# Conditional layer and quantised FFN on one core: where the weights' powers are formed, a GpSimd product and a bound matmul moved

## The chip, the cores and the metric

The kernel runs on one core of one Trainium2 chip. The metric is the device time of the whole program in microseconds (us); lower is better. TensorE (PE in the profile) does the matrix products, VectorE (DVE), ScalarE (ACT) and GpSimd (POOL) the element-wise work, and SyncE (SP) issues the transfers. SBUF is the on-chip memory, PSUM the smaller one that TensorE writes.

## The reference

```python
# x (64, 64, 1024): batch, channel, feature; condition (64,) in 0..15; weights (16, 64, 64)
W = weights[condition]
h = einsum('bct,bcd->bdt', x, W)                    # first product: one 64x64 matrix a batch
w = (unpack6(qweight) - zero_point) * scale         # (1024, 1024), 6-bit integers, one zero point
                                                    # and one scale for each output feature
out = x + einsum('bsk,nk->bsn', h, w) + bias        # second product, bias and residual
```

All tensors are float32, the packed weights int32.

## The kernel before

**Tiling.** Two batches make a pair: 2 x 64 channels lie on the 128 partitions, with the 1024 features along the free axis. There are 32 pairs, and two pairs make a group. For each pair, `stage1` computes h into a PSUM tile `ph` (features on partitions, the channels of both batches along the free axis), and `stage2` multiplies it with the unpacked integers `q` (`qT`) into the PSUM tile `po` (128 x 1024, two banks of 512). Both operands of a product are float16. Precision is kept by splitting each value into a high and a low half: `hh` and `hl` for h, `hf`/`lf` stacked as `xa` for x, a high and a low table `tab` for the weights. So the second product of a pair is 32 matmuls of 128x512 columns: 8 feature tiles, two halves (`hh`, `hl`), two banks.

**Powers.** Values are scaled by a power of two before they are split. `powers(sums, up, down)` (L130 to L138) takes a bound that TensorE has put in PSUM and writes two tiles: `down`, the inverse power by which the operand is multiplied, and `up`, the power that is multiplied back. For the weights of each condition, `weights_powers` makes `wdn` and `wup`, both in SBUF, from the PSUM tile `pw`; `weights_scaled` (GpSimd) multiplies the weights by `wdn`; `weights_high` (ScalarE) and `weights_low` (VectorE) make the table `tab` of it. `weights_hot` and `weights_of_batches` bring `wup` of every batch's condition to the tile `wupb`: a diagonal product `up_k` of `wup` and the identity `eye`, a reduction `up_1`, a row tile `up_w`, an indicator `hot`, and one matmul. `wupb` enters the factor `u` of a group (`unscales`), with which `po` is multiplied at the end.

**Zero point.** The zero point's share is `zt = zero point * sum over features of h` for each pair, made by ScalarE. From pair 4 on it uses `zsc` = zero point times scale, one product on GpSimd (L633), and GpSimd subtracts it from the residual. Pairs 0 to 3 (`early_zero_points`, `early_minus`, `early_res`, `early_add`) use the plain zero point on VectorE: `early_minus` is po * u - zt in PSUM, `early_res` multiplies by the scale into an SBUF tile `res`, and GpSimd adds that later.

**PSUM.** `po` has two buffers, one for even and one for odd pairs; a pair's second product waits until the pair two before has been read out of its buffer. All small matmul results (`pw`, `pl`, `pu`, `pt`, `pb_`) share one pool of two buffers.

**Order.** The order on each engine is written out by hand; each engine executes its own queue in order, and the calls in the program are its order. The main loop `window(p)` covers pairs from 3 on. Ahead of it stands a start-up in which the weights' tables don't exist yet: pairs 0 and 1 run their first product in float32 with plain weights `wbd` (`early_stage1`, bounds by `early_bounds`, powers by `early_scales`, halves by `early_high` and `early_low`). In the meantime the integers are unpacked (`unpack`, VectorE), the table is built, and group 1 (pairs 2 and 3) is prepared: `stacked_high` (ScalarE) and `stacked_low` (VectorE, reads x and `xa`) write `xa` directly, where later groups go through SBUF and transfers (`split_1`, `split_2`, `stack_high`, `stack_low`). `select_pair(n, nc.gpsimd)` copies the two weight matrices of a pair out of `tab` into `wst`; `stage1(n)` reads that. The end of the start-up, in the order of the calls:

```python
    weights_low()
    ...
    for n in range(2, 4):
        select_pair(n, nc.gpsimd)
    nc.gpsimd.tensor_tensor(zsc, zsb, scb, ALU.mult)
    for n in range(4, 8):
        select_pair(n, nc.gpsimd)
```

Of the kernel before, what the change touches and what calls it, by code (L numbers as in the profile page):

```python
# [8 lines left out]
F32 = mybir.dt.float32  # L9
F16 = mybir.dt.float16  # L10
BF = mybir.dt.bfloat16
# [3 lines left out]
ALU = mybir.AluOpType  # L15
AX = mybir.AxisListType
# [13 lines left out]
def adaln_ffn(ctx: ExitStack, tc: tile.TileContext, x, cond, cw, qw, ws, wz, bias, out):  # L30
    nc = tc.nc
    B, C, T = x.shape
    _, NK, D = cw.shape
    N = qw.shape[2]
    P = 128
    NP = B // 2
    NG = NP // 2
    KT = T // P
# [6 lines left out]
    const = ctx.enter_context(tc.tile_pool(name="const", bufs=1))  # L45
# [34 lines left out]
    cb = const.tile([NK, B], I32, name="cb")  # L80
# [39 lines left out]
    spread = const.tile([NK, P], BF, name="spread")  # L120
# [3 lines left out]
    kio = const.tile([NK, 1], F32, name="kio")  # L124
# [3 lines left out]
    eye = const.tile([P, P], BF, name="eye")  # L128
    nc.vector.tensor_scalar(eye, off, 0, None, ALU.is_equal)

    def powers(sums, up, down, least=True):

        if least:
            nc.vector.tensor_scalar(sums, sums, LEAST, None, ALU.max)
        nc.vector.tensor_scalar(
            down.bitcast(I32), sums.bitcast(I32), EXPONENT, EXPONENT, ALU.bitwise_and, ALU.bitwise_xor
        )
        nc.vector.tensor_scalar(up.bitcast(I32), sums.bitcast(I32), EXPONENT, None, ALU.bitwise_and)  # L138
# [5 lines left out]
    def unpack(kt, n=1):  # L144

        w = kt if kt < 2 else kt - 2 if kt < 6 else kt - 4
        to, of_ = q16[:, kt : kt + n, :], qr[:, w : w + n, :]
        if kt in (2, 3, 6, 7):
            nc.vector.tensor_scalar(to, of_, 6 if kt < 4 else 8, 63, ALU.logical_shift_right, ALU.bitwise_and)
        else:  # L150
            nc.vector.tensor_scalar(to, of_, 63, None, ALU.bitwise_and)


    tab = const.tile([P, NK, 2, D], F16, name="tab")
    wup = const.tile([P, NK], F32, name="wup")
    wupb = const.tile([P, NP], F32, name="wupb")
    wdn = const.tile([P, NK], F32, name="wdn")
    wsc = qp.tile([P, NK, D], F32, name="wsc", bufs=1)
    wmx = const.tile([C, NK], BF, name="wmx")
    tmp = {}  # L160
# [4 lines left out]
    def weights_turn():  # L165
        pt = ps_s.tile([NK, C], F32, name="pt", tag="s")
        nc.tensor.matmul(pt, lhsT=wmx, rhs=eye[LO, LO], start=True, stop=True)
        tmp["pt"] = pt

    def weights_diagonal():  # L170
        most = const.tile([NK, 1], F32, name="most")
        nc.vector.tensor_reduce(most, tmp["pt"], AX.X, ALU.max)
        diag = const.tile([NK, NK], BF, name="diag")
        nc.vector.tensor_scalar(diag, eye[0:NK, 0:NK], most[:, 0:1], None, ALU.mult)
        tmp["diag"] = diag
# [4 lines left out]
        tmp["pw"] = pw  # L180

    def weights_powers():
        powers(tmp["pw"], wup, wdn)

    def weights_scaled():
        nc.gpsimd.tensor_tensor(wsc, w32, wdn.unsqueeze(2).to_broadcast([P, NK, D]), ALU.mult)  # L186
# [4 lines left out]
    def weights_low():  # L191
        nc.vector.tensor_tensor(tab[:, :, 1, :], wsc, tab[:, :, 0, :], ALU.subtract)

    def weights_hot():

        hot = const.tile([NK, B], BF, name="hot")
        nc.vector.tensor_scalar(hot, cb, kio[:, 0:1], None, ALU.is_equal)
        up_k = const.tile([NK, NK], F32, name="up_k")
        nc.vector.tensor_tensor(up_k, wup[0:NK, :], eye[0:NK, 0:NK], ALU.mult)
        up_1 = const.tile([NK, 1], F32, name="up_1")  # L200
        nc.vector.tensor_reduce(up_1, up_k, AX.X, ALU.add)
        up_w = const.tile([NK, P], BF, name="up_w")
        nc.vector.tensor_scalar(up_w, spread, up_1[:, 0:1], None, ALU.mult)
        tmp["hot"] = up_w, hot

    def weights_of_batches():
        up_w, hot = tmp["hot"]
        pb_ = ps_s.tile([P, B], F32, name="pb_", tag="s")
        nc.tensor.matmul(pb_, lhsT=up_w, rhs=hot, start=True, stop=True)
        for j, h in enumerate((LO, HI)):  # L210
            nc.vector.tensor_scalar(
                wupb[h], pb_.rearrange("p (i j) -> p i j", j=2)[h, :, j], 1.0 / LARGEST, None, ALU.mult
            )
# [4 lines left out]
    def conditions_of(p, eng=nc.sync):  # L218
        conditions[p] = [
            eng.value_load(cb[0:1, 2 * p + j : 2 * p + j + 1], min_val=0, max_val=NK - 1) for j in range(2)  # L220
        ]

    def select_pair(p, eng=nc.sync):
        g, i = divmod(p, 2)
        if i == 0:
            wsts[g] = sp.tile([P, 2, 2, 2, D], F16, name="wst")
        if p not in conditions:
            conditions_of(p, eng)
        for j, k in enumerate(conditions[p]):
            to, of_ = wsts[g][:, i, :, j, :], tab[:, ds(k, 1), :, :].rearrange("p o a d -> p (o a) d")  # L230
            if eng is nc.sync:
                eng.dma_start(to, of_)
            else:
                eng.tensor_copy(to, of_)
# [9 lines left out]
    def magnitudes(g, i):  # L244
        if g not in st:
            st[g] = {
                "l1": sp.tile([P, 2], BF, name="l1"),
                "u": sp.tile([P, 2], F32, name="u"),
                "hs": sp.tile([P, 2], F32, name="hs"),
                "xs": sp.tile([P, 2], F32, name="xs"),  # L250
                "up": sp.tile([P, 2], F32, name="up"),
                "down": sp.tile([P, 2], F32, name="down"),
                "hf": ap.tile([P, 2, T], F16, name="hf"),
                "lf": ap.tile([P, 2, T], F16, name="lf"),
                "xa": ap.tile([P, 2, 2, T], F16, name="xa"),
            }
        junk = ap.tile([P, T], BF, name="junk", bufs=1)
        nc.scalar.activation(junk, xts[g][:, i, :], AF.Abs, accum_out=st[g]["l1"][:, i : i + 1])  # L258
# [9 lines left out]
    def unscales(g):  # L268
        nc.vector.scalar_tensor_tensor(st[g]["u"], st[g]["up"], 0.25 / QUNIT, wupb[:, 2 * g : 2 * g + 2], ALU.mult, ALU.mult)
# [112 lines left out]
    def early_weights(p):  # L382

        wl = const.tile([P, 1], F32, name=f"wl{p}")
        nc.vector.tensor_reduce(wl, wbd[:, p, :], AX.X, ALU.max, apply_absolute_value=True)
        nc.vector.tensor_scalar(wm[:, p, :], half, wl[:, 0:1], None, ALU.mult)
# [17 lines left out]
    def early_bounds(p, parts):  # L404
        pl = ps_s.tile([P, 2], F32, name="pl", tag="s")
        for n in range(parts):
            nc.tensor.matmul(pl, lhsT=all_ones, rhs=pb[:, p, n, :], start=(n == 0), stop=(n == parts - 1))  # L407
        tmp["pl"] = pl
# [4 lines left out]
    def early_unscales(p):  # L413
        for j, h in enumerate((LO, HI)):
            nc.vector.tensor_scalar(st[0]["u"][h, p : p + 1], updown[h, p, 0, j : j + 1], 0.5 / QUNIT, None, ALU.mult)

    def early_stage1(p, ph, kts=range(KT)):
        for kt in kts:
            nc.tensor.matmul(  # L419
                ph[:, kt % ph.shape[1], :, :], lhsT=xts[0][:, p, ts(kt, P)], rhs=wbd[:, p, :], start=True, stop=True  # L420
            )
# [22 lines left out]
    def early_zero_points(p):  # L444
        g, i = divmod(p, 2)
        zt = ap.tile([P, N], F32, name="zt", bufs=3)
        nc.scalar.activation(zt, zsb, AF.Copy, scale=st[g]["hs"][:, i : i + 1])  # L447
        tmp["zt", p] = zt
# [64 lines left out]
    def stage2_tiles(p, kts, ks=range(2)):  # L513
        if p not in pos:
            pos[p] = ps_o[1 + p % 2].tile([P, N], F32, name="po", tag="po")
        products(pos[p], p, kts, ks, BANKS, BANKS)
# [50 lines left out]
    ph1 = ps_o[0].tile([P, KT, 2, D], F32, name="ph")  # L567
# [12 lines left out]
    early_rows(0, 0)  # L580
    early_rows(0, 1)
    early_stage1(0, ph0b, range(4, KT))
    early_stage1(1, ph1, range(0, 2))
    early_bounds(0, 2)
    early_scales(0)
    early_high(0, ph0a, LOWER)
    early_high(0, ph0b, UPPER)
    early_weights(1)
    early_stage1(1, ph1, range(2, KT))
    unpack(0)  # L590
    unpack(1)
    early_low(0, ph0a, LOWER)
# [3 lines left out]
    early_low(0, ph0b, UPPER)  # L596
    weights_turn()
    weights_diagonal()
    unpack(4, 2)
    stage2_tiles(0, range(0, 2), [1])  # L600
    early_rows(1, 0)
# [5 lines left out]
    early_bounds(1, 1)  # L607
    early_scales(1)
    weights_powers()
    weights_scaled()  # L610
    magnitudes(1, 0)
    early_high(1, ph1, slice(0, KT))
    stage2_tiles(0, range(4, 6))
# [11 lines left out]
    early_feature_sums(1)  # L625
    magnitudes(1, 1)
    early_zero_points(0)
    weights_low()
    unpacking.close()
    late = ctx.enter_context(tc.tile_pool(name="late", bufs=1))  # L630
    for n in range(2, 4):
        select_pair(n, nc.gpsimd)
    nc.gpsimd.tensor_tensor(zsc, zsb, scb, ALU.mult)  # L633
    for n in range(4, 8):
        select_pair(n, nc.gpsimd)


# [1 line left out]
    stage2_tiles(1, range(0, 4), [1])  # L639
    bounds(1, SECOND)  # L640
    scales(1, SECOND)
    early_unscales(0)
    early_unscales(1)
    weights_hot()
    early_minus(0)
    early_res(0)
    stage2_tiles(1, range(4, 7))
# [10 lines left out]
    stacked_low(1, 1, 1)  # L658
    weights_of_batches()
    unscales(1)  # L660


    sums_high(1)
# [167 lines left out]
```

## Time and profile before

| what | us |
|---|---|
| median of 3 runs | 271.44 (270.45 to 272.37) |
| the profiled execution | 271.85 |
| its span, first to last instruction | 270.1 |
| mean granted TensorE clock | 0.993 of full |
| a pair in the steady part (from one `stage1` to the next, 93.11 to 100.95) | 7.84 |

The profile is of one execution. Its span is what the instructions cover; the 1.75 us between span and time lie around it. An engine's row gives its busy time, its share of the span and its number of instructions. Lines of a timeline give the start in us, the duration, the engine, the line of the program, the operation, the output and inputs by their names, the count, and, in brackets, how long the engine was idle before it and what released it. Lines of the list of waits read: total us, times, longest. Lines of windows give the stretch, its length, the busy time of PE, PEld, DVE, ACT and POOL with their instructions, the granted clock, the share of the DMA engines and GB/s.

### The profile page before, as it was taken

How to read it: one execution, taken by the hardware profiler on the slowest of the kernel's cores; microseconds unless marked ns; L12 is line 12 of the kernel's file. 1: busy time of each engine (PE TensorE's matmuls, PEld its weight loads, DVE VectorE, ACT ScalarE, POOL GpSimd, SP SyncE). 2: the span in 40 equal slices, each digit the busy share in tenths (PEclk: the TensorE clock that was granted, in tenths of full speed). 3: DMA queues.
4: the chain of work that ended last, by engine and by line, in shares of the span. 5: the costliest groups of instructions: out<-in, count | busy, mean ns of one | idle time of the engine just before them, and what ended most of it. 6: DMA issues, size and time to landing. Idle time of an engine off the chain costs nothing.

```text
span 270.1 us, 5703 instructions
## 1 busy us (share of the span) xinstructions
PE 261.8 (97%) x2158; PEld 139.9 (52%) x2158; DVE 204.1 (76%) x269; ACT 161.2 (60%) x287; POOL 172.2 (64%) x100
## 2 busy tenths in 40 slices
PE   7997899999999999999999999999999999999993
PEld 7554446445555545555554555555455555545553
DVE  4779999597795959869595986959598695955543
ACT  3799399776565667656566765656676565634100
POOL 3027017959599595969959596895919386595100
PEclk9999799999999999999999999999999999999999
DMA  6993047966667797596965797667966664551212
GB/s 213 341 407 132 1 94 234 268 178 187 198 175 245 225 281 219 120 317 176 302 184 175 233 273 231 174 230 248 272 220 187 203 179 144 161 158 78 80 53 103
DMA packets 31820, 53.34 MB, mean 197 GB/s; under 512 B 15024, under 2 KB 15280, under 8 KB 31792
## 3 DMA queue, kind: packets, MB, share of 16 engines
q1 hardware_dynamic: 31760, 52.96, 63.9%
q8 instruction: 17, 0.28, 0.4%
q14 instruction: 11, 0.09, 0.1%
q10 hardware_dynamic: 32, 0.00, 0.0%
HBM read 19.93 MB, written 16.78 MB: 136 GB/s over the span
## 4 chain that ended last, share of the span: by engine, by line
PE 94%; DMA 2%; DVE 1%; SPq 1%; ACT 0%; issue 0%
PE po L503 80%; PE ph L479 10%; PE pe L503 3%; DMA xt<-in_x_dram 2%; PE ph L419 1%; PE pu L350 1%; DVE po L452 0%; DVE res L458 0%; SPq L65 0%; SPq L86 0%; ACT hh L491 0%; DVE pe L544 0%; DVE xt L549 0%; PE pu L441 0%; PE pl L407 0%
## 5 line engine op out<-in xcount | busy, mean ns | idle before, releaser
L503 PE MATMUL po<-q,hh 128*128 128x512 f16 x496 | 120.0, 382 | 2.3 <-DVE res L458 2.3
L503 PE MATMUL po<-q,hl 128*128 128x512 f16 x496 | 118.5, 379 | 0.0
L539 POOL TENSOR_TENSOR xt<-xt,zt 128x1024 f32<-128x1024 f32 x28 | 78.5, 2822 | 49.3 <-ACT zt L537 49.3
L503 PEld LDWEIGHTS <-hl 128*128 128x128 f16 x520 | 50.8, 98 | 59.8 <-issue 0.4
L491 ACT CAST hh<-ph 128x1024 f16<-128x1024 f32 (+1 forms) x31 | 30.4, 984 | 83.7 <-PE ph L479 41.9
L503 PEld LDWEIGHTS <-hh 128*128 128x128 f16 x520 | 48.7, 98 | 54.9 <-ACT zt L447 2.4
L532 POOL TENSOR_TENSOR xt<-xt,bib 128x1024 f32<-128x1024 f32 x32 | 74.5, 2355 | 1.9 <-issue 1.9
L544 DVE SCALAR_TENSOR_TENSOR po<-po,u,scb 128x1024 f32<-128x1024 f32 x27 | 34.7, 1286 | 49.6 <-PE po L503 49.6
L292 DVE SCALAR_TENSOR_TENSOR lf<-xt,down,hf 128x1024 f16<-128x1024 f32 x28 | 60.1, 2184 | 0.2 <-ACT hf L282 0.2
L495 DVE TENSOR_TENSOR hl<-ph,hh 128x1024 f16<-128x1024 f32 x30 | 36.4, 1215 | 0.1
L479 PEld LDWEIGHTS <-xa 128*128 128x128 f16 x960 | 32.2, 98 | 7.2
L549 DVE TENSOR_TENSOR xt<-po,xt 128x1024 f32<-128x1024 f32 x27 | 33.1, 1225 | 1.9
L479 PE MATMUL ph<-wst,xa 128*128 128x64 f16 x960 | 33.0, 193 | 0.0
L258 ACT ACTIVATE junk<-xt 128x1024 bf16<-128x1024 f32 x30 | 31.7, 1056 | 0.8
L282 ACT ACTIVATE hf<-xt,down 128x1024 f16<-128x1024 f32 x28 | 31.9, 1143 | 0.0
L537 ACT ACTIVATE zt<-zsc,hs 128x1024 f32<-128x1024 f32 x28 | 30.5, 1138 | 0.0
L343 ACT ACTIVATE xh<-xh,xs 64x1 f16<-64x1 f16 x52 | 12.4, 287 | 0.5
L468 POOL TENSOR_TENSOR xt<-xt,res 128x1024 f32<-128x1024 f32 x4 | 9.4, 2360 | 0.0
L339 POOL TENSOR_TENSOR xh<-xs,xh 64x2 f16<-64x2 f32 x4 | 0.8, 194 | 10.7 <-ACT xh L333 10.6
L186 POOL TENSOR_TENSOR wsc<-w,wdn 128x1024 f32<-128x1024 f32 x1 | 1.9, 1902 | 8.3 <-DVE wup L138 8.3
L503 PE MATMUL pe<-q,hh 128*128 128x256 f16 (+1 forms) x24 | 6.6, 308 | 0.0
L503 PE MATMUL pe<-q,hl 128*128 128x256 f16 (+1 forms) x24 | 6.5, 308 | 0.0
(88 smaller groups left out, 123.4 us busy)
## 6 DMA issues: line engine op xcount, KB each, us to landing
out_dram<-xt SPq DMA_DIRECT2D x31, 512.0 KB, 3.0
xt<-in_x_dram SPq DMA_DIRECT2D x14, 1024.0 KB, 7.9
xa<-hf SPq DMA_DIRECT2D x26, 256.0 KB, 3.8
xa<-lf SPq DMA_DIRECT2D x26, 256.0 KB, 3.8
xt<-in_x_dram SPq DMA_DIRECT2D x3, 512.0 KB, 7.8
wst<-tab SPq DMA_DIRECT2D x48, 32.0 KB, 3.2
w<-in_L_cond_weights_dram SPq DMA_DIRECT2D x2, 256.0 KB, 5.9
xt<-in_x_dram SPq DMA_DIRECT2D x2, 256.0 KB, 3.7
```

The lines of the kernel that those rows point to most:

```text
L258: nc.scalar.activation(junk, xts[g][:, i, :], AF.Abs, accum_out=st[g]["l1"][:, i : i + 1])
L282: nc.scalar.activation(st[g]["hf"][:, i, ts_], xts[g][:, i, ts_], AF.Copy, scale=st[g]["down"][:, i : i + 1], accum_out=st[g]["xs"][:, i : ...
L292: nc.vector.scalar_tensor_tensor(st[g]["lf"][:, i, ts_], xts[g][:, i, ts_], st[g]["down"][:, i : i + 1], st[g]["hf"][:, i, ts_], ALU.mult, ...
L479: nc.tensor.matmul(ph[:, kt, j, :], lhsT=st[g]["xa"][:, i, j, ts(kt, P)], rhs=wsts[g][:, i, a, j, :], start=(a == 0), stop=(a == 1),)
L491: nc.scalar.copy(hs_pair[p][0][:, kts, :], ph[:, kts, :])
L495: nc.vector.tensor_tensor(hl[:, kts, :], ph[:, kts, :], hh[:, kts, :], ALU.subtract)
L503: nc.tensor.matmul(po[:, a], lhsT=hs_pair[p][k][:, kt, :], rhs=qT[:, kt, c], start=(kt == 0 and k == 0), stop=(kt == KT - 1 and k == 1),)
L532: nc.gpsimd.tensor_tensor(xt, xt, bib, ALU.add)
L537: nc.scalar.activation(zt, zsc, AF.Copy, scale=st[g]["hs"][:, i : i + 1])
L539: nc.gpsimd.tensor_tensor(xt, xt, zt, ALU.subtract)
L544: nc.vector.scalar_tensor_tensor(po, po, st[g]["u"][:, i : i + 1], scb[:, cols], ALU.mult, ALU.mult)
L549: nc.vector.tensor_tensor(xts[g][:, i, cols], po, xts[g][:, i, cols], ALU.add)
```

## The change

`wup` is no longer written to SBUF: `weights_powers` forms that power in place, in the PSUM tile `pw`, and `weights_own`, called right behind `weights_scaled`, multiplies the diagonal and reduces it there. What was one function `weights_hot` becomes three, called at different places: `weights_hot` (the indicator) behind `weights_diagonal`, `weights_own`, and `weights_up` (the row tile) ahead of `weights_low`. `early_unscales(0)` moves ahead of `weights_low`, `early_unscales(1)` behind `unscales(1)`. GpSimd's `zsc` product comes after the copies of pair 2, ahead of those of pair 3, instead of after both. On TensorE, `early_bounds(0, 2)` comes ahead of all eight feature tiles of `early_stage1(1, ph1)`, instead of after the first two.

```diff
-    wup = const.tile([P, NK], F32, name="wup")
...
     def weights_powers():
-        powers(tmp["pw"], wup, wdn)
+
+        powers(tmp["pw"], tmp["pw"], wdn)
...
     def weights_hot():
 
-        hot = const.tile([NK, B], BF, name="hot")
-        nc.vector.tensor_scalar(hot, cb, kio[:, 0:1], None, ALU.is_equal)
-        up_k = const.tile([NK, NK], F32, name="up_k")
-        nc.vector.tensor_tensor(up_k, wup[0:NK, :], eye[0:NK, 0:NK], ALU.mult)
-        up_1 = const.tile([NK, 1], F32, name="up_1")
-        nc.vector.tensor_reduce(up_1, up_k, AX.X, ALU.add)
-        up_w = const.tile([NK, P], BF, name="up_w")
-        nc.vector.tensor_scalar(up_w, spread, up_1[:, 0:1], None, ALU.mult)
-        tmp["hot"] = up_w, hot
+        tmp["hot"] = const.tile([NK, B], BF, name="hot")
+        nc.vector.tensor_scalar(tmp["hot"], cb, kio[:, 0:1], None, ALU.is_equal)
+
+    def weights_own():
+
+        up_k = tmp["pw"][0:NK, :]
+        nc.vector.tensor_tensor(up_k, up_k, eye[0:NK, 0:NK], ALU.mult)
+        tmp["up_1"] = const.tile([NK, 1], F32, name="up_1")
+        nc.vector.tensor_reduce(tmp["up_1"], up_k, AX.X, ALU.add)
+
+    def weights_up():
+        tmp["up_w"] = const.tile([NK, P], BF, name="up_w")
+        nc.vector.tensor_scalar(tmp["up_w"], spread, tmp["up_1"][:, 0:1], None, ALU.mult)
 
     def weights_of_batches():
-        up_w, hot = tmp["hot"]
+
         pb_ = ps_s.tile([P, B], F32, name="pb_", tag="s")
-        nc.tensor.matmul(pb_, lhsT=up_w, rhs=hot, start=True, stop=True)
+        nc.tensor.matmul(pb_, lhsT=tmp["up_w"], rhs=tmp["hot"], start=True, stop=True)
...
     early_stage1(0, ph0b, range(4, KT))
-    early_stage1(1, ph1, range(0, 2))
     early_bounds(0, 2)
     early_scales(0)
     early_high(0, ph0a, LOWER)
     early_high(0, ph0b, UPPER)
     early_weights(1)
-    early_stage1(1, ph1, range(2, KT))
+    early_stage1(1, ph1)
...
     weights_diagonal()
+    weights_hot()
     unpack(4, 2)
...
     weights_scaled()
+    weights_own()
     magnitudes(1, 0)
...
     early_zero_points(0)
+    early_unscales(0)
+    weights_up()
     weights_low()
...
-    for n in range(2, 4):
-        select_pair(n, nc.gpsimd)
+    select_pair(2, nc.gpsimd)
     nc.gpsimd.tensor_tensor(zsc, zsb, scb, ALU.mult)
-    for n in range(4, 8):
+    for n in range(3, 8):
         select_pair(n, nc.gpsimd)
...
     scales(1, SECOND)
-    early_unscales(0)
-    early_unscales(1)
-    weights_hot()
     early_minus(0)
...
     unscales(1)
+    early_unscales(1)
```

## The prediction

> **What bounds the kernel now.** I read the page's busy shares first, then the list of waits of TensorE, then the timelines of TensorE, VectorE and GpSimd around the one long wait, then the windows there. The chance bounds below use 1% (2.7 us), about what a measurement of this kernel can tell from no change.
>
> ```profile
> PE 261.8 (97%) x2158; PEld 139.9 (52%) x2158; DVE 204.1 (76%) x269; ACT 161.2 (60%) x287; POOL 172.2 (64%) x100
> ...
> PEclk9999799999999999999999999999999999999999
> ```
>
> TensorE is busy 97% of the 270.1 us span, so time can only come from its gaps or from its clock. The clock digit falls once, in the fifth slice (27.0 to 33.8 us). The list of TensorE's waits holds three entries:
>
> ```profile
> PE po L503 <- DVE res L458: 2.3, 1, 2.3
> PE pc L562 <- DVE one L106: 1.1, 1, 1.1
> PE ph L419 <- DMA xt<-in_x_dram: 0.8, 2, 0.5
> ```
>
> The last two lie before 7.7 us (start-up, first loads). The first is the target: pair 2's second product waits until `early_res(0)` has read pair 0's PSUM, which both pairs use in turn. TensorE's timeline there:
>
> ```profile
> 25.40 0.20 PE L209 MATMUL pb__625<-hot,up_w 16*128 16x64 bf16 x1
> 27.92 3.41 PE L503 MATMUL po<-q,hh 128*128 128x512 f16 x8 [2.31 <-DVE res L458]
> 31.16 1.89 PE L503 MATMUL po<-q,hl 128*128 128x512 f16 x8
> ```
>
> Eight hh matmuls take 3.24 us from start to start (27.92 to 31.16), where eight hl take 1.73 (31.16 to 32.89). The windows say why:
>
> ```profile
> 27.90:31.20 3.30, 3.28 (x9) 1.19 (x10) 3.24 (x3) 1.46 (x5) 0.39 (x2) 0.52 0.00 0
> 31.20:32.90 1.70, 1.70 (x10) 0.76 (x9) 1.62 (x5) 0.00 (x0) 0.00 (x0) 1.00 0.00 0
> ```
>
> Column seven is the granted clock: 0.52 behind the gap, 1.00 after. So the wait costs twice: 2.3 us idle and 3.24 - 1.73 = 1.5 us of half clock. Why VectorE is late, from its timeline and GpSimd's:
>
> ```profile
> 22.48 2.34 DVE L199 TENSOR_TENSOR up_k<-wup,eye 16x16 f32<-16x16 f32 x1
> 24.86 0.16 DVE L201 TENSOR_REDUCE up<-up_k 16x1 f32<-16x16 f32 x1
> 25.06 0.26 DVE L203 TENSOR_SCALAR up_w<-spread,up 16x128 bf16<-16x128 bf16 x1
> 25.24 1.27 DVE L452 SCALAR_TENSOR_TENSOR po<-po,u,zt 128x1024 f32<-128x1024 f32 x1
> 26.55 1.23 DVE L458 TENSOR_TENSOR res<-po,scb 128x1024 f32<-128x1024 f32 x1
> ...
> 22.45 2.35 POOL L633 TENSOR_TENSOR zsc<-zsb,scb 128x1024 f32<-128x1024 f32 x1
> ```
>
> A 16x16 product, where other tiny operations take some 0.16, lasts 2.34 us: exactly GpSimd's zsc product (22.45 to 24.80). VectorE then runs in order: up_1, up_w, `early_minus(0)`, `early_res(0)`, and TensorE starts 0.14 after res.
>
> **What the Trainium skill says.** "SBUF — State Buffer", section "Who interferes with whom": a VectorE instruction with two SBUF inputs contends with a GpSimd instruction that reads SBUF, and the second to start blocks fully; with at most one SBUF input (outside its two-port modes) it doesn't. The trace agrees: up_k reads wup and eye, both in SBUF, and lasts as long as zsc, while `early_minus(0)` (PSUM and SBUF) beside GpSimd's copies takes its plain 1.27. "TensorE: Matmul & The Clock Gate", section "What's actually happening", lets the clock halve after an idle window of about 3.4 us; here 2.3 us of idling sufficed for about 3.3 us at half. So I take small waits as free of it and anything near 2 us as at risk.
>
> **The change part by part.**
>
> *Powers in PSUM (`weights_powers`, `weights_own`).* The write of wup becomes an in-place write of pw, one instruction for one (0.16). up_k and the reduction move from 22.5 to behind wdn's power at 14.2, on the same VectorE queue. up_k there has one SBUF input (eye), at most 0.2, and the reduction takes 0.16. VectorE idles 1.18 us until 15.56 at that place, waiting for `bounds(1, FIRST)`, so 0.4 is hidden; uncovered it would cost those 0.4. The tile pw is held until about 14.8; the next tile in its buffer is written at 15.33. Bounds: 0 to 0.4, taken 0.
>
> *hot* (0.24, pitch 0.16) moves ahead of unpack(4, 2). VectorE is full there (9.06 to 13.7), but see the next edit: 0.
>
> *Bound of pair 0 ahead of pair 1's first product.* Its inputs are ready at 6.99 (row L402), TensorE is free at 7.19 and idles till 7.68 for pair 1's load. So the two bound matmuls (8.20 now) run at about 7.2 in that gap, and the powers, `early_high(0)` and VectorE's unpacking come up to 1 us sooner. On TensorE itself only the 0.06 that these took disappears: everything from 7.68 to 25.3 is matmul behind matmul. If the inputs were late, pair 1's product would wait behind them; 0.2 of slack. Taken -0.07.
>
> *early_unscales(0) and weights_up* move from behind `scales(1, SECOND)` to ahead of `weights_low`: two at 0.155 and one at 0.18 make 0.5. Queued behind them: `weights_low` (20.20 now, 20.6 then, tab ready at 21.86), so GpSimd's copies for pair 2 end at 22.4, where stage1(2) starts at 23.5: hidden. Also `scales(1, SECOND)`, 0.43 later, and so ScalarE's stacked_high(1, 1): 21.73 becomes 22.16, ending at 24.66; stage1_high(2) starts at about 24.7 instead of 24.64. No TensorE time.
>
> *zsc ahead of pair 3's copies.* GpSimd: tab 21.9, two copies to 22.4, zsc to 24.7, ten copies at 0.24 to 27.2. Pair 3's are wanted at 29. No DMA and nothing of SP moves in any part.
>
> *The sum.* VectorE after scales(1, SECOND) at 22.1: minus(0) to 23.4, res(0) to 24.65. TensorE, without the wait for up_w and 0.07 earlier, is ready for pair 2's product at about 25.4, so the wait for res goes and the clock stays up. What is late next is hl of pair 2: stacked_low(1, 1, 0), two SBUF inputs, begins at 24.67 at the very end of zsc (24.7) and among copies of 0.24; then stage1_low(2), 1.26. It ends at 27.2 with no contention, at 27.5 with one copy ahead; TensorE wants it at 25.4 + 1.73 = 27.1 and starts 0.14 after its end. So hl begins at 27.35 to 27.65 instead of 31.16: 3.5 to 3.8 gained. Behind it: stacked_low(1, 1, 1) ends at 28.5 to 28.9 for stage1(3) at 29.1 to 29.4. early_unscales(1) (0.31, now behind unscales(1)) and minus(1) end at 30.7, 0.6 after the bounds(2) matmul (30.1), but ScalarE's stage1_high(3) ends only at 31.0, so split_1(2, 0) loses 0.1. split_2(2, 0) runs at 32.85, some 0.4 later against TensorE than now; its DMAs (issue to landing 2.2 to 2.4) had 0.3 of slack to stage1(4) at 40.86. So another 0.1 to 0.2 may be lost there. I take 3.6: the profiled execution (271.85, 1.75 around its span) becomes 268.25. The shown median is 271.44, 0.4 lower; less 3.6 it is 267.8.
>
> **The rivals.**
>
> *Forecast (0.62):* the wait and the half clock go, small new waits of 0.2 to 0.9 remain: gain 3.0 to 3.9, 267.5 to 268.4. For it: every one of the steps above has its row. Against: the new margins are a few tenths.
>
> *The wait turns into one for hl of pair 2 (0.20):* more copies of GpSimd get ahead of stacked_low(1, 1, 0), or both of the two-input operations block, and hl starts 1 to 2 us late with some of the half clock: gain 1.2 to 2.7, about 269.5. For it: in the steady windows the second `split_2` lasts up to 3.44 instead of 1.28 beside GpSimd's products. Against: a copy is 0.24, not 2.35, and the lock changes hands after each instruction there.
>
> *Slower (0.08):* GpSimd keeps its read interface through all ten copies, 2.4 us. Place: stacked_low(1, 1, 0). hl would end at 29.7, TensorE idle from 27.1 to 29.85 and again at half clock for 1.55: pair 2's first bank ends at 33.1 instead of 32.89, 271.7. It decides from a wait of about 2.3 us on; a second such wait with its clock loss at stage1(4), as VectorE's lag reaches the DMAs, would bring 274 and over (half of this chance).
>
> *It doesn't do what it says (0.06):* the in-place power in PSUM still blocks, or res(0) waits for something else in its memory: about 271.
>
> *More (0.04):* also the other executions lose more in that gap than the profiled one: 266.8.
>
> **How the numbers follow.** The forecast's 267.8, median against median. The range leaves out the worst of the slower and the best of the rest: 266.6 to 270.3. Faster by over 1% means below 268.7: nearly all of the forecast, the last case, a few of the second: 0.68. Slower by over 1%: 0.04. Within: 0.28.
>
> **What would show it.** Right: TensorE's list of waits without res L458; clock 1.00 from 25 to 32; up_k some 0.17 long at 14.5; res(0) ending at 24.7; po of pair 2 starting at 25.4; hl beginning near 27.5; from stage1(4) on the same 7.9 us a pair, some 3.6 earlier. Wrong: a stacked_low above 1.6 us, a low clock digit after 25 us, a new wait for hl, xa or a DMA of over 0.7 us.

## The result, and the profile after

The changed kernel takes 268.75 us (median of 5, 267.94 to 269.37) where the kernel before, run beside it, takes 271.86 (median of 5, 270.45 to 272.58): 3.1 us less, ratio 0.989 with a 95% interval of 0.9851 to 0.9928. A second comparison (e11 below) gave 268.26 against 271.73, ratio 0.9863 (0.9824 to 0.9901). The forecast was 3.6 less.

The page of the profiled execution (269.19 us, span 267.4):

```profile
PE 260.4 (97%) x2158; PEld 139.5 (52%) x2158; DVE 200.1 (75%) x269; ACT 161.2 (60%) x287; POOL 174.6 (65%) x100
...
PEclk9999999999999999999999999999999999999999
```

TensorE's share is still 97%, the low clock digit is gone, and VectorE is busy 4 us less with as many instructions: the time in which an instruction stands blocked counts as busy, and up_k alone gave back 2.2. Most of the rest is the product that makes `lf` in the steady part (60.1 us in all before, 58.0 now). TensorE's entries in the list of waits:

```profile
PE ph L423 <- DMA xt<-in_x_dram: 1.2, 3, 0.6
PE pc L566 <- DVE one L106: 1.1, 1, 1.1
PE ph L483 <- DMA xa<-lf: 0.6, 1, 0.6
```

The wait for res is not there. A new one is: `stage1(6)` waits for its stacking transfer. TensorE's timeline at the old and at the new place, and two windows (the clock is the seventh column):

```profile
25.96 0.20 PE L213 MATMUL pb__621<-hot,up_w 16*128 16x64 bf16 x1
26.09 1.90 PE L507 MATMUL po<-q,hh 128*128 128x512 f16 x8
27.87 1.90 PE L507 MATMUL po<-q,hl 128*128 128x512 f16 x8
...
49.93 0.22 PE L483 MATMUL ph<-wst,xa 128*128 128x64 f16 x2
50.76 1.03 PE L483 MATMUL ph<-wst,xa 128*128 128x64 f16 x30 [0.61 <-DMA xa<-lf]
```

```profile
26.00:28.00 2.00, 2.00 (x11) 0.86 (x11) 1.94 (x3) 1.98 (x3) 2.00 (x7) 1.00 0.02 8
28.00:30.00 2.00, 2.00 (x22) 1.07 (x21) 1.87 (x6) 1.92 (x6) 1.69 (x4) 1.00 0.00 0
```

Pair 2's product follows the matmul of `weights_of_batches` after 0.13 instead of 2.52 us, at full clock; its hh half takes 1.78 from start to start. In this execution the load of pair 1 landed 0.7 us later than in the one shown before, so everything up to here stands 0.56 later (pair 0's second product starts at 10.24 instead of 9.68). hl starts 3.29 earlier, 3.85 if that is taken off; of this the wait at stage1(6) gives back about 0.7. VectorE and GpSimd:

```profile
14.99 0.17 DVE L202 TENSOR_TENSOR pw<-pw,eye 16x16 f32<-16x16 f32 x1
...
22.59 1.28 DVE L456 SCALAR_TENSOR_TENSOR po<-po,u,zt 128x1024 f32<-128x1024 f32 x1
23.91 1.23 DVE L462 TENSOR_TENSOR res<-po,scb 128x1024 f32<-128x1024 f32 x1
25.16 1.39 DVE L319 SCALAR_TENSOR_TENSOR xa<-xt,down,xa 64x1024 f16<-64x1024 f32 x1
26.59 1.23 DVE L499 TENSOR_TENSOR hl<-ph,hh 128x1024 f16<-128x1024 f32 x1
...
22.89 2.37 POOL L639 TENSOR_TENSOR zsc<-zsb,scb 128x1024 f32<-128x1024 f32 x1
25.19 4.40 POOL L238 COPY wst<-tab 128x128 f16 x10
```

up_k, the product of pw with eye, takes 0.17 us; res ends at 25.14, ahead of TensorE's need at 26.09. The two-input stacked_low right behind zsc lasts 1.39 instead of 1.28, so it lost 0.1, and hl ends at 27.82, just when TensorE wants it. The blocking has changed sides: GpSimd's ten copies take 4.40 us, at 0.24 each they would take 2.4. Two of them, at 25.42 and at 28.08, stand for 1.29 and 1.28 us, about as long as the two products of stacked_low that they meet.

### The profile page after: what moved, and what is told of

The parts are those of the page before. It is cut to its first block, busy times and chain, and to the rows that moved or that the text cites. A ratio compares the mean times of both kernels' runs of the same rounds, so it can differ in the third digit from the quotient of the medians.

```text
span 267.4 us, 5704 instructions
## 1 busy us (share of the span) xinstructions
PE 260.4 (97%) x2158; PEld 139.5 (52%) x2158; DVE 200.1 (75%) x269; ACT 161.2 (60%) x287; POOL 174.6 (65%) x100
## 4 chain that ended last, share of the span: by engine, by line
PE 82%; DVE 9%; DMA 4%; issue 1%; ACT 1%; SPq 1%; DVEq 0%
PE po L507 69%; PE ph L483 9%; PE pe L507 3%; DMA xa<-lf 2%; DMA xt<-in_x_dram 2%; DVE lf L296 2%; DVE xa L319 1%; DVE hl L499 1%; DVE po L456 1%; ACT xa L311 1%; DVE res L462 1%; PE ph L423 1%; DVE hl L438 0%; PE pu L354 0%; DVE tab L192 0%
## 5 line engine op out<-in xcount | busy, mean ns | idle before, releaser
L507 PE MATMUL po<-q,hh 128*128 128x512 f16 x496 | 118.4, 379 | 0.0
L296 DVE SCALAR_TENSOR_TENSOR lf<-xt,down,hf 128x1024 f16<-128x1024 f32 x28 | 58.0, 2108 | 0.0
L238 POOL COPY wst<-tab 128x128 f16 x12 | 4.9, 454 | 5.5 <-DVE tab L192 5.5
```

Of the source, the lines that this page charges most:

```text
L296: nc.vector.scalar_tensor_tensor(st[g]["lf"][:, i, ts_], xts[g][:, i, ts_], st[g]["down"][:, i : i + 1], st[g]["hf"][:, i, ts_], ALU.mult, ...
L507: nc.tensor.matmul(po[:, a], lhsT=hs_pair[p][k][:, kt, :], rhs=qT[:, kt, c], start=(kt == 0 and k == 0), stop=(kt == KT - 1 and k == 1),)
```

## The experiments

Each kernel ran beside the kernel before; those of one group (e1 to e4; e5 to e8; e9 to e11; e12) on one chip.

| run | us, median | before | ratio, 95% interval |
|---|---|---|---|
| e1 zsc late only | 268.86 | 272.50 | 0.9878 (0.9840 to 0.9915) |
| e2 gap filled | 270.98 | 272.50 | 0.9951 (0.9934 to 0.9967) |
| e3 power in SBUF | 267.97 | 272.50 | 0.9843 (0.9811 to 0.9875) |
| e4 one load early | 268.22 | 272.50 | 0.9845 (0.9814 to 0.9876) |
| e5 zsc at its old place | 268.61 | 272.10 | 0.9870 (0.9841 to 0.9899) |
| e6 bound at its old place | 268.64 | 272.10 | 0.9876 (0.9846 to 0.9907) |
| e7 one product more | 269.48 | 272.10 | 0.9902 (0.9865 to 0.9938) |
| e8 two products more | 270.99 | 272.10 | 0.9954 (0.9939 to 0.9970) |
| e9 two loads early | 267.96 | 271.73 | 0.9843 (0.9808 to 0.9878) |
| e10 the same, zsc late | 268.79 | 271.73 | 0.9875 (0.9840 to 0.9911) |
| e11 the changed kernel | 268.26 | 271.73 | 0.9863 (0.9824 to 0.9901) |
| e12 three products more | 272.75 | 271.82 | 1.0023 (1.0005 to 1.0040) |

**e1: is the lock the cause?** The kernel before, with one line moved.

```diff
-    nc.gpsimd.tensor_tensor(zsc, zsb, scb, ALU.mult)
...
     sums_low(1, nc.gpsimd)
+    nc.gpsimd.tensor_tensor(zsc, zsb, scb, ALU.mult)
```

Expected: 

> The kernel before with one edit: GpSimd's zsc product goes behind the zero-point sums of group 1 (about 30 us), so nothing with two SBUF inputs meets it; wup stays in SBUF, up_k and everything else stay where they are. Theory 1 (the 2.3 us wait comes from up_k blocked by zsc): up_k falls from 2.34 us to 0.2 to 0.5 (a copy of GpSimd may still be ahead), early_res(0) ends at 25.5 to 25.9 instead of 27.78, no half clock, then a wait for hl of pair 2 of 0.6 to 1.0: gain 2.5 to 3.2 us, nearly all of the change's 3.1. Theory 2 (the gain comes from the shorter work of VectorE ahead of early_minus(0) and the earlier bound, the lock is incidental): up_k stays above 1.5 us or the gain is below 1 us.

Measured: 3.6 us less than before; 2.5 to 3.2 was expected. From VectorE's and TensorE's timelines of e1:

```profile
22.46 0.26 DVE L199 TENSOR_TENSOR up_k<-wup,eye 16x16 f32<-16x16 f32 x1
24.44 1.23 DVE L458 TENSOR_TENSOR res<-po,scb 128x1024 f32<-128x1024 f32 x1
...
28.29 1.90 PE L503 MATMUL po<-q,hl 128*128 128x512 f16 x8 [0.59 <-DVE hl L495]
```

The same up_k, at the same place, with the same two inputs in SBUF, takes 0.26 instead of 2.34 us once zsc is away. That is theory 1, and the move of this one line brings as much as the whole change, within the intervals; what the rest of the change saves on VectorE shows here as the wait of 0.59 for hl.

**e2: does the gap cost a second time?** The kernel before, with dummy matmuls in the gap.

```diff
     early_minus(1)
+    fill = ps_s.tile([P, P], F32, name="fill", tag="s")
+    for _ in range(38):
+        nc.tensor.matmul(fill, lhsT=dummy, rhs=dummy, start=True, stop=True)
     stage2_bank(2, 0)
```

Expected: 

> The kernel before with 38 dummy matmuls of 128x128 (about 2.1 us, result unused) put on TensorE into the gap between the matmul of weights_of_batches and pair 2's second product; the wait for early_res(0) stays. Theory 1 (the wait costs twice, by idling and by the half clock behind it): the clock stays at 1.00 from 27.9 to 31.2, eight hh take 1.73 instead of 3.24 us, and the gain is about 1.5 us minus a wait for hl of pair 2 that now shows (hl ends at 30.34, wanted at 29.65: 0.8): 0.5 to 1.5 us. Theory 2 (the half clock is of the time of the run, or of the operands, not of the gap): the low clock stays and nothing is gained, or up to 0.1 is lost.

Measured: 1.5 us less. TensorE's timeline of e2:

```profile
25.18 2.29 PE L668 MATMUL fill<-dummy 128*128 128x128 bf16 x38
27.56 1.89 PE L503 MATMUL po<-q,hh 128*128 128x512 f16 x8
30.04 1.90 PE L503 MATMUL po<-q,hl 128*128 128x512 f16 x8 [0.59 <-DVE hl L495]
```

With TensorE kept busy through the gap, hh runs at full speed and then waits for hl. Without the dummies the half clock had covered that wait. The mean granted clock of every execution says more. In the kernel before, over all its 88 executions in the four groups, it is 0.990 to 0.994 in 53 (median 272.74 us) and 0.997 to 1.0 in 35 (median 271.46); nothing lies between. With the gap filled all 18 executions are at 0.997 or above. So the half clock belongs to the gap, but it comes in about three executions of five only, and by the medians of the two groups it costs 1.3 us where it comes.

**e3: need the power be in PSUM?** The changed kernel with wup in SBUF again, read at the new place.

```diff
-        powers(tmp["pw"], tmp["pw"], wdn)
+        tmp["wup"] = const.tile([P, NK], F32, name="wup")
+        powers(tmp["pw"], tmp["wup"], wdn)
...
-        up_k = tmp["pw"][0:NK, :]
+        up_k = tmp["wup"][0:NK, :]
```

Expected: 

> The changed kernel, but the weights' power is written to an SBUF tile again, and weights_own reads it there, at its new place; all else as changed. Theory 1 (with two SBUF inputs up_k meets whatever GpSimd reads): up_k starts at 15.0 together with wsc (15.01, 1.9 us) and either slips in ahead of it (0.17 us, wsc 0.2 later, no cost) or is blocked to 16.9; then the powers of bounds(1, FIRST) come at 17.1 instead of 16.13, ScalarE and VectorE are 0.8 to 1 us late, and TensorE waits 0.8 to 1 us at stage1(2) or at pair 2: gain against before 2.0 to 2.5 instead of 3.1. Theory 2 (only the place counts, not the memory): up_k 0.2 us, time as the changed kernel within 0.3 us.

Measured: 267.97, no slower than the changed kernel. VectorE's and GpSimd's timelines of e3:

```profile
14.47 0.16 DVE L203 TENSOR_TENSOR wup<-wup,eye 16x16 f32<-16x16 f32 x1
...
14.50 1.90 POOL L187 TENSOR_TENSOR wsc<-w,wdn 128x1024 f32<-128x1024 f32 x1 [8.11 <-DVE wup L138]
```

up_k starts 0.03 us ahead of the product it could have been blocked by, and is not blocked. Nor is wsc: the two overlap by 0.13 us, and it lasts 1.90 us as it does in the kernel before and in the changed one. Theory 1's first branch had wsc 0.2 later, which did not come; so this meeting doesn't show the blocking at all, and fits theory 2. What it says of the change: the new place was enough here, and the operand in PSUM is a safeguard against a loss that did not occur. The reverse, the operand in PSUM at the old place, was not run.

**e4 and e9: the new wait at stage1(6).** The changed kernel with the transfers of x for group 4 (e4), or groups 4 and 5 (e9), issued at the start.

```diff
     nc.sync.dma_start(bib, bias.partition_broadcast(P))
+    load_x(4)
+    load_x(5)                      # e9 alone
...
     magnitudes(3, 1)
-    load_x(4)
...
-            if g + 3 < NG:
+            if g + 3 < NG and g > 2:   # e9 alone: group 5 is not loaded again
```

Expected, e4: 

> The changed kernel, but the transfer of x for group 4 (1 MB) is issued behind the bias at about 10.6 us, instead of at 38.3 us behind the stacking transfers of group 2. Theory 1 (the 0.7 us wait of TensorE at stage1(6), 50 us, is the stacking transfer of pair 6 and 7 queued behind this load): that transfer lands in 2.3 to 4 us instead of 6.0, the wait goes, 0.5 to 0.7 us are gained on the changed kernel (267.9 to 268.2). Theory 2 (the transfer is long by itself or for another load): it still takes 5 to 6 us, the wait stays. Theory 3: the early load delays the rest of the start-up's loads (bias, x of group 3): a new wait before 30 us, slower than the changed kernel.

Expected, e9: 

> The changed kernel with the transfers of x for groups 4 and 5 (1 MB each) issued behind the bias, at about 13 us, instead of at 38.3 and 45.4 us. Theory 1 (the stacking transfers of pairs 6 and 7 take 4.5 to 6 us because the load of group 5 runs beside them): they land in 2.3 to 3.5 us, no wait at stage1(6): 0.1 to 0.7 us gained on the changed kernel, 268.0 or so. Theory 2 (the four stacking transfers, 1 MB in all, take that time by themselves): 4.5 us and more still, the wait comes and goes by run.

Measured: 268.22 and 267.96. In e4 the wait is 0.15, with the transfers of `lf` landing 5.1 to 5.2 us after their issue; in e9 the list of waits shows none, but there they still take 4.6 to 5.5, with no load beside them. In the changed kernel's two profiles it was 5.4 to 6.0 with a wait of 0.61, and 4.7 to 5.1 with none (e11). So theory 2 of both: the four stacking transfers, 1 MB in all and issued within 3 to 4 us, take some 5 us on their own. The last is issued about 5 us ahead of stage1(6) (5.3 in the changed kernel, 44.63 to 49.93), and a wait of 0 to 0.8 us comes and goes by execution (0.78 in e6). In the kernel before it was as close: its transfer landed at 53.3 and the product, due at 53.21, ran its first two matmuls and then 30 from 53.44. The median of e9 is 0.3 us below that of e11, the changed kernel beside it, which the intervals do not separate.

**e5: the place of zsc, in the changed kernel.**

```diff
-    select_pair(2, nc.gpsimd)
+    for n in range(2, 4):
+        select_pair(n, nc.gpsimd)
     nc.gpsimd.tensor_tensor(zsc, zsb, scb, ALU.mult)
-    for n in range(3, 8):
+    for n in range(4, 8):
```

Expected: 

> The changed kernel with zsc back behind the copies of both pairs 2 and 3; all else as changed. Theory 1 (with up_k out of its reach, zsc matters only for stacked_low(1, 1, 0)): zsc runs about 0.5 us later, to 25.2 in the time of a run whose first load lands at 7.5; stacked_low(1, 1, 0), ready at 24.65, is blocked 0.5 to 0.6 and lasts 1.8 to 2.0 us instead of 1.39; TensorE waits 0.4 to 0.6 us for hl of pair 2, no half clock: gain against before 0.5 less than the changed kernel's. Theory 2 (the move of zsc is what counts): 1.5 us or more of the gain are lost.

Measured: 268.61, not separable from the changed kernel. VectorE's and TensorE's timelines of e5:

```profile
24.96 1.65 DVE L319 SCALAR_TENSOR_TENSOR xa<-xt,down,xa 64x1024 f16<-64x1024 f32 x1
...
27.93 1.90 PE L507 MATMUL po<-q,hl 128*128 128x512 f16 x8
```

stacked_low is 0.26 longer than the 1.39 with zsc moved, and hl starts 2.03 after hh (25.90) instead of 1.78. Theory 1 holds at half its expected size: at this place, moving zsc ahead of two copies is worth 0.25 us, too little for the time to show it.

**e6: the place of the bound.**

```diff
     early_stage1(0, ph0b, range(4, KT))
+    early_stage1(1, ph1, range(0, 2))
     early_bounds(0, 2)
...
-    early_stage1(1, ph1)
+    early_stage1(1, ph1, range(2, KT))
```

Expected: 

> The changed kernel with two feature tiles of pair 1's first product ahead of the bound of pair 0 again; all else as changed. Theory 1 (the bound's place saves no time of TensorE, since everything from 7.7 to 25 us is matmul behind matmul): ScalarE's early_high(0) about 0.7 to 1 us later, pair 0's second product at the same distance from the last first product, time as the changed kernel within 0.3 us. Theory 2 (the earlier bound brings VectorE's start-up forward, and some of the gain): 0.5 us or more lost.

Measured: 268.64, between the two medians of the changed kernel (268.26 and 268.75), as theory 1 has it. ScalarE's early_high(0) starts 1.0 us ahead of pair 0's second product here (8.51 and 9.52), 1.75 in the changed kernel (8.49 and 10.24): the bound's place does bring ScalarE forward by some 0.75, as expected. Little of it arrives at TensorE: hl of pair 2 starts 1.89 after hh here (25.37 and 27.26), 1.78 in the changed kernel, so 0.1 us.

**e7, e8, e12: how long a gap?** The changed kernel with one, two or three products ahead of early_minus(0).

```diff
     scales(1, SECOND)
+    slow = late.tile([P, N], F32, name="slow")
+    nc.vector.tensor_tensor(slow, pos[0], tmp["zt", 0], ALU.mult)    # once, twice or three times
     early_minus(0)
```

Expected, e7: 

> The changed kernel with one product of 128x1024 (1.25 us, result unused) added on VectorE ahead of early_minus(0), so that early_res(0) ends about 1.25 us later. Theory 1 (a short wait costs itself alone, the half clock needs a longer gap): TensorE idles 0.7 to 0.9 us for res and 0.3 to 0.5 for hl, 1.2 to 1.3 in all, clock 1.00 throughout, 1.2 to 1.3 us slower than the changed kernel. Theory 2 (any gap of about 1 us brings the half clock): 1.5 us more.

Expected, e8: 

> The changed kernel with two such products (2.5 us) ahead of early_minus(0). Theory 1: TensorE idles about 2.1 us for res, as in the kernel before, the half clock follows for some 3.3 us and costs 1.5; hl is then no further wait: 3.4 to 3.9 us slower than the changed kernel, so about the kernel before. Theory 2 (the half clock of before had to do with something else there): no half clock, 2.5 us slower.

Expected, e12: 

> The changed kernel with three added products (3.7 us) ahead of early_minus(0). So far the kernel before, with a gap of 2.3 us in one piece, ran at a mean clock of 0.990 to 0.994 in 40 of 61 executions and at 0.997 to 1.0 in 21; with two added products, with gaps of 1.5 and 0.6, none of 20 executions was below 0.997. Theory 1 (the half clock comes by chance and the more often the longer the gap is): a gap of about 2.7 us for res, and 0.6 for hl in the executions that keep the clock; more than two thirds of the executions at 0.994 or below; 271.9 with the clock kept, about 273 with it lost. Theory 2 (the half clock belongs to something else in the kernel before): no execution below 0.996.

Measured: 269.48, 270.99 and 272.75. The same line of TensorE's timeline, pair 2's first and second half, in e7, e8 and e12:

```profile
25.97 1.89 PE L507 MATMUL po<-q,hh 128*128 128x512 f16 x8 [0.25 <-ACT hh L495]
28.61 1.90 PE L507 MATMUL po<-q,hl 128*128 128x512 f16 x8 [0.76 <-DVE hl L499]
```

```profile
27.90 1.89 PE L507 MATMUL po<-q,hh 128*128 128x512 f16 x8 [1.51 <-DVE res L462]
30.38 1.90 PE L507 MATMUL po<-q,hl 128*128 128x512 f16 x8 [0.59 <-DVE hl L499]
```

```profile
28.91 1.89 PE L507 MATMUL po<-q,hh 128*128 128x512 f16 x8 [2.76 <-DVE res L462]
31.39 1.90 PE L507 MATMUL po<-q,hl 128*128 128x512 f16 x8 [0.59 <-DVE hl L499]
```

The idle time grows with the delay, 1.0, 2.1 and 3.35 us. At 1.0 the cost over the changed kernel's two medians is 0.7 to 1.2 us, at 2.1 it is 2.2 to 2.7: about the idling alone. At 2.1, in two pieces, none of 20 executions falls below 0.997 of the clock, so theory 1 of e8 was wrong in this; its theory 2 named another reason, which e12 takes away. With 2.76 in one piece 16 of 22 are at 0.992 to 0.994 (the profiled one is among the others), as e12's theory 1 expected. That 2.8 us bring the half clock more often than 2.3 (53 of 88 in the kernel before) is not shown, for the shares are too close; that 1.5 us bring it less often (0 of 20) is. e12 is slower than the kernel before by 0.23% (0.05 to 0.40%) and e8 faster, so a delay of VectorE between 2.5 and 3.7 us undoes the change: about 3.1 by a straight line between their medians, 1.1 less and 0.9 more.

What decides whether the clock falls can be read in the traces. In the profiled execution of the kernel before it falls at 27.62 us, returns at 31.04 and falls again at 269.97, when the matmuls are over. These times are 3.41 and 238.93 us apart, 1 and 70 times 3.413. In each of the other 13 profiles the clock stays up for one stretch of 259.41 or 262.83 us: 76 and 77 times 3.413. So the clock changes on a grid of 3.413 us, and the profiles show the grid at different places against the program. One step at half clock takes 0.006 from the mean clock of 270 us, which is what sets the group at 0.990 to 0.994 apart. Windows of the kernel before and of e12 along its steps (the figure behind the length is TensorE's busy time, the clock is the seventh column):

```profile
24.21:27.62 3.41, 1.39 (x19) 0.62 (x15) 3.31 (x5) 2.97 (x5) 2.49 (x9) 1.00 0.01 2
27.62:31.04 3.42, 3.12 (x8) 1.17 (x9) 3.32 (x4) 1.74 (x6) 0.39 (x2) 0.50 0.01 2
31.04:34.45 3.41, 3.41 (x50) 2.10 (x48) 2.72 (x8) 0.43 (x1) 0.00 (x0) 1.00 0.03 5
```

```profile
23.77:27.19 3.42, 2.38 (x40) 1.42 (x37) 3.35 (x4) 3.31 (x7) 3.42 (x10) 1.00 0.04 16
27.19:30.60 3.41, 1.69 (x8) 0.71 (x8) 3.31 (x4) 2.71 (x7) 0.84 (x4) 1.00 0.01 2
```

In the kernel before TensorE idles for 2.02 us of the step ahead of the fall. In e12 the gap is longer, but a step ends inside it, at 27.19, and leaves 1.04 us on one side and 1.72 on the other; this execution kept its clock. In all 14 profiles, the ends of the programs taken in, the clock fell behind every step at full clock with 2.02 us of idling or more, and behind none with 1.72 or less. An estimate from these figures: if the limit lies between 1.72 and 2.02 and a gap falls anywhere on the grid alike, the share of places at which one step holds that much of it is (3.41 + gap - 2 x limit) / 3.41. A gap of 2.31 us would then bring the half clock in 49 to 67% of the executions, one of 2.76 in 62 to 80%, one of 1.51, shorter than the limit, never. Measured were 60, 73 and 0%. So the half clock looks like chance only as long as the place of the gap on the grid is not known.

**e10: zsc out of the way altogether.** e9 with the line moved as in e1.

Expected: 

> The same, and zsc behind the zero-point sums of group 1 (about 30 us), the candidate for a version ahead of both kernels. stacked_low(1, 1, 0) meets copies of 0.24 alone: 1.3 to 1.5 us; hl of pair 2 ends 0.1 us sooner at most, where TensorE waited 0.05. Theory 1 (nothing is left in this stretch but matmuls): within 0.3 us of the run with the loads alone. Theory 2 (the copies of GpSimd, stretched to 4.4 us by the alternation, held something up): 0.3 us or more gained.

Measured: 268.79, 0.8 above e9 where an equal or a lower time was expected. The intervals against the kernel before overlap, but all six executions of e10 (268.40 and more) lie above all six of e9 (268.36 and less). Neither theory has the reason that the profile shows. VectorE's, GpSimd's and TensorE's timelines of e10:

```profile
31.12 1.31 DVE L275 SCALAR_TENSOR_TENSOR u<-up,wupb 128x2 f32<-128x2 f32 x1
...
30.06 2.35 POOL L670 TENSOR_TENSOR zsc<-zsb,scb 128x1024 f32<-128x1024 f32 x1
...
36.31 1.90 PE L509 MATMUL po<-q,hl 128*128 128x512 f16 x8 [0.44 <-DVE hl L501]
```

It is the same trap, two columns wide: `unscales(2)` multiplies two SBUF tiles of 128x2, meets zsc, and ends with it at 32.43 instead of after 0.16 us. Pair 3's hl comes late and TensorE waits. In e1, with zsc at the same place, this product starts 0.6 us ahead of zsc's end and lasts 0.59: that nothing with two SBUF inputs would meet zsc there was expected, and did not hold. In the place that the change gives it, zsc runs beside early_minus(0) and early_res(0), which read PSUM and one SBUF tile and are not touched. No run gave a version that is clearly ahead of the changed kernel.

**e11: the changed kernel again.** Expected: 

> The changed kernel once more, beside the other two on the same chip: 268.0 to 269.4, a wait at stage1(6) of 0 to 0.7 us.

Measured: 268.26 (267.53 to 269.46), no wait at stage1(6) in its profile.

## Why the prediction was right

**What bounds, and the cause: right.** up_k was blocked by zsc: without zsc beside it, 0.26 us (e1); without a second SBUF input and at an earlier place, 0.17; at the earlier place alone, 0.16 (e3). The wait for res disappeared in both. The rule of the Trainium skill ("SBUF — State Buffer", section "Who interferes with whom"), that a VectorE instruction with two SBUF inputs contends with a GpSimd instruction that reads SBUF, held for up_k (2.34 us), for stacked_low and even for the 128x2 product of e10 (1.31). The operations with one PSUM input kept their plain times: early_minus takes 1.28 us beside zsc and 1.27 in the kernel before. Only in e3, where the two overlap by 0.13 us, neither is longer.

**The steps.** With the 0.56 of the later load added, the prediction's times stand as follows: res ending at 25.2 (measured 25.14), pair 2 starting at 25.96 (26.09), hl between 27.9 and 28.2 (27.87), split_2(2, 0) at 33.4 (33.27), no wait at stage1(4) (none). stacked_low was priced at up to one copy of 0.24 extra and took 0.11 extra. The parts costed at nothing show none in the timelines: the in-place power takes 0.17 us where the write to SBUF took 0.16, and hot 0.23 instead of 0.24. The bound, taken at 0.07, is worth 0.1 at hl (e6).

**The size: 3.1 and 3.5 us measured, 3.6 forecast.** Up to hl the profiled execution gained 3.85, a little more than the 3.5 to 3.8 of the sum. Two terms were mis-sized. The wait at stage1(6), for which the sum had nothing, took back 0.7 in that execution and nothing in e11's. And the half clock was counted in full, 1.5 us, from one execution. It comes in 53 of 88 executions, and it also covered a wait for hl: without it, hh would have ended at 27.92 + 1.73 = 29.65, while hl was written at 30.34, so 0.7 of the 1.5 was lost either way (e2 shows that wait, 0.59). So an execution of the kernel before that keeps its clock should leave some 0.7 us less to gain. The medians of the two groups, 272.74 and 271.46, differ by 1.3 (in e12 by 0.6); where the rest arises stays open, since no profile shows the kernel before with its clock kept. The medians of the kernel before in the groups, 271.73 to 272.50, differ by 0.8 among themselves, and the forecast's 267.8 started from one of 271.44, of three executions. That the size came so near is therefore in part luck.

**The rivals.** The wait that turns into one for hl was real in kind and 0.05 us in size; the steady windows' alternation, which spoke against it, is what the copies show too (4.40 us for ten: GpSimd waited, not VectorE). The slower one was to decide from a delay of about 2.3 us on; e8 and e12, which delay early_minus(0) instead of stacked_low, put the point near 3.1. That the clock loss was counted as certain there too is one reason; a delay of stacked_low itself was not run. The new wait that did come, the stacking transfers of pair 6, was looked for at stage1(4), one group too early.

## What to carry to other kernels

A tiny instruction that lasts as long as another engine's large one is likely to be blocked, not slow: look at what runs beside it, and move either one, or give the small one an operand in PSUM. Before moving the large one, list the two-SBUF-input instructions of VectorE in its new window, however small they are. A gap on TensorE can cost more than its length, but price that second cost from the clocks of many executions, look where the gap lies between the times at which the clock can change, and subtract what the slower stretch was hiding.

## What the runs showed of the hardware that was not expected

The half clock behind a gap is not decided by the program alone: the same kernel with the same 2.3 us gap kept its clock in 35 of 88 executions, and with a gap of 2.76 us in 6 of 22. Gaps of 1.5 and 0.6 us with 1.9 us of matmuls between them left all 20. In the 14 profiles the clock changes on a grid of 3.413 us; it fell behind the steps in which TensorE idled for 2.02 us or more, and behind none with 1.72 or less. And the size of an instruction doesn't protect it from being blocked: a product of 128x2, which takes 0.16 us by itself, stood for 1.31 beside GpSimd's product (e10).
